# A window attention kernel whose values lie in DRAM with chunks and channels innermost, stored in pieces by two engines

## The chip, the core and the metric

The kernel runs on one core of a Trainium2 chip. The core has five engines that run side by side and are kept in step by semaphores: TensorE (PE) multiplies matrices, VectorE (DVE), ScalarE (ACT) and GpSimd (POOL) work on elements, and SyncE (SP) issues transfers. Transfers between SBUF (on the chip, 128 partitions) and DRAM are carried out by 16 DMA engines. The metric is the device time of one execution, in microseconds (us), where less is better.

## The reference

The input is 16 images of 64 x 64 positions with 256 channels, float32. Two layers run one after the other, each as `x = x + layer(groupnorm(x))`:

```python
# layer 0: linear attention, 8 heads of 32 channels
q, k, v = split(gn(x) @ w_qkv)
q = softmax(q, over a head's channels) * SCALE;  k = softmax(k, over all positions)
x = x + ((k @ v^T) @ q) @ w_out
# layer 1: each position attends to the 7 x 7 positions around it, zero padded
q, k, v = gn(x) @ Wq + bq, gn(x) @ Wk + bk, gn(x) @ Wv + bv
scores = q . (k_window + emb);   x = x + softmax(scores) . v_window
```

The values of layer 1 are what this change is about: `v` is computed for all positions, and every position needs the values of its 49 neighbours, with zeros beyond the image's edge.

## The kernel before, in words

The images are worked through one after the other, in four stages. (1) `layer0` does the linear attention. (2) The group norm of layer 1 is folded into the weights; `positional` computes terms for the position embedding, `store_rings` writes them to DRAM (L658), and `values` computes the values strip by strip and stores them to DRAM (L677, L680, L685, L690). (3) `keys_queries` computes keys and queries for a half of the heads (`hg`), and PSUM is emptied by ACT and DVE into `kaug` and `qq` (L703, L619, L621). (4) `local_attention` computes scores, exponentials and the weighted sums (L760, L768, L791) for that half. Stages 3 and 4 run twice.

The 4096 positions are kept in eight strips of 512. Seven of them are blocks of 8 columns by 64 rows, shifted by 3 so that they match the units of the window scheme. Strip 0 holds the image's two edges, 5 columns on the left and 3 on the right; `block_order` puts these into four groups of 16 rows, within a group the 5 left columns first.

Values go through DRAM because a product with the values needs positions in the partitions in another arrangement than the one in which they are computed. `vpad` is zero padded and has nine units of 8 columns, 72 rows each (nine chunks of 8 rows). Strip `s` is stored as unit `s` by one DMA of 512 KB. Strip 0 belongs to the units 0 and 8 and is stored by eight small DMAs (L690). The zeros around the image are written once, at the start, by 40 small DMAs (L399 to L401). There are two `vpad`, for even and odd images.

`load_window` brings the two units that a step of the attention needs back into SBUF, as `vw`. A DMA moves one unit and one half of the channels: 64 partitions (the 64 positions of a chunk), and for each of them nine chunks with 128 channels (288 KB, in runs of 512 B). Four such DMAs make a window, and two windows are in flight.

The order on PE, ACT, DVE and SP is the order of the program text (`manual_schedule`), so an engine that waits holds up all that follows on it. Around the change it is, for one image: `positional`; the bias of the values; `store_rings` (16 DMAs on SP); `values` for the strips 2, 3, 4, 5, then `load_rings(0)` (8 DMAs on SP, L665 and L666), then `values` for 6, 7, 1, 0; the folding of the key and query biases (L612 on PE, L614 on DVE); two windows loaded; a half of the next image loaded (L463); `keys_queries`; `local_attention`.

Value tiles come from a pool of four buffers that the other stages use too (`work`). A tile that takes a buffer waits until the buffer's last user is done, a store included:

```python
work = ctx.enter_context(tc.tile_pool(name="work", bufs=4))
v4 = work_tile(f"v4_{b}_{s}")
```

The DMAs of the program use eight completion semaphores in turn. A DMA is issued only when the one eight places before it in the program's order has landed.

Of the kernel before, what the change touches and what calls it, by code (L numbers as in the profile page):

```python
# [10 lines left out]
F32 = mybir.dt.float32  # L11
# [8 lines left out]
P = 128  # L20
W = 64
# [19 lines left out]
UNITS = (1, 2, 3, 0)  # L41
KEYED = (2, 3, 4, 5, 6, 7, 1, 0)
ORDER = (3, 4, 5, 6, 7, 1, 2, 0)
EDGE = (5, 3)


def block_order():

    pos = np.arange(NT).reshape(W, W)
    edge = [pos[16 * g : 16 * g + 16, a:e].ravel() for g in range(4) for a, e in ((0, EDGE[0]), (W - EDGE[1], W))]  # L50
    inner = [pos[:, 8 * u - PAD : 8 * u - PAD + 8].ravel() for u in range(1, NB - 1)]
    return np.concatenate(edge + inner)

# [6 lines left out]
def shape_constants():  # L60

    p = np.arange(P)
    c = np.zeros((P, C_COLS), np.float32)
    c[:, C_GRP : C_GRP + P] = (p[:, None] // 8 == p[None, :] // 8) / 8.0
    slot = p % 64
    r = np.arange(RING)
    off = (slot[:, None] - r[None, :]) % RING
    for hg in range(2):
        dyn = (slot >= 32 + 16 * hg) & (slot < 48 + 16 * hg)
        sel = (off[:, :, None] == np.arange(KS)) & dyn[:, None, None]  # L70
        c[:, C_DSEL + 112 * hg : C_DSEL + 112 * (hg + 1)] = sel.reshape(P, -1)
# [10 lines left out]
    blocks = onehot.reshape(2 * RING, WP, NB, 8).transpose(0, 2, 1, 3).reshape(2 * RING, -1)  # L82

    far = np.where((np.arange(RING)[:, None] - np.arange(W)[None]) % RING >= KS, -BIG, 0.0)
    ring = np.broadcast_to(far[:, None, :], (RING, W, W)).reshape(RING, NT)
    return c, onehot, np.ascontiguousarray(blocks), ring.astype(np.float32)


class Net:
# [266 lines left out]
def attention_fast(tc, io, ok):  # L356
# [3 lines left out]
    with ExitStack() as ctx:  # L360
# [28 lines left out]
        xc, xt, out, vpad, pos = io["xc"], io["xt"], io["out"], io["vpad"], io["pos"]  # L389
        B = xc.shape[0]  # L390
        with tc.tile_pool(name="zeros", bufs=1) as zp:
            zero = zp.tile([P, 8 * C], F32, tag="zero", name="zero")
            nc.gpsimd.memset(zero, 0.0)
            last = WP - PAD - W
            for v in vpad:
                rows = v.rearrange("a r w c -> a r (w c)")
                for r0, m in ((0, PAD), (WP - last, last)):
                    for a in range(NB):
                        nc.sync.dma_start(rows[a, r0 : r0 + m], zero[:m])  # L399
                nc.sync.dma_start(v[0, PAD : PAD + W, :PAD].rearrange("r w c -> r (w c)"), zero[:W, : PAD * C])  # L400
                nc.sync.dma_start(v[NB - 1, PAD : PAD + W, PAD:].rearrange("r w c -> r (w c)"), zero[:W, : last * C])  # L401
            far = zp.tile([W, 8 * C], F32, tag="far", name="far")
            nc.gpsimd.memset(far, -BIG)
            for d in pos:
                for i in range(2):
                    part = d[:, RING + 8 * i : RING + 8 * i + 8].rearrange("a s h w -> a (s h w)")
                    nc.sync.dma_start(part, far)
# [8 lines left out]
        for k in kaug:  # L416
            for ab in range(2):
                nc.gpsimd.memset(k[64 * ab : 64 * ab + 32], 0.0)
                nc.sync.dma_start(k[64 * ab + 32 : 64 * ab + 64].rearrange("p a b c -> p (a b c)"), io["blocks"])
        w2 = cp.tile([P, 2, C], F32, tag="w2", name="w2")  # L420


# [59 lines left out]
        def pieces(s):  # L482


            if s:
                yield s, 0, 8, 8 * s - PAD, lambda a: a.rearrange("p (r w) -> p r w", w=8)
                return
            for u, p0, m, n0, w in ((0, PAD, EDGE[0], 0, 0), (NB - 1, 0, EDGE[1], 16 * EDGE[0], W - EDGE[1])):

                def view(a, m=m, n0=n0):  # L490
                    part = a.rearrange("p (g n) -> p g n", g=4)[:, :, n0 : n0 + 16 * m]
                    return part.rearrange("p g (r w) -> p g r w", w=m)

                yield u, p0, m, w, view

        def by_rows(a, like):

            return a.rearrange("p (g r) w -> p g r w", g=4) if len(like.shape) == 4 else a

        def layer0(b, x, xn, mean, rstd, xtok, ready):  # L500

# [136 lines left out]
        def positional(i, pair):  # L638


            for a in range(2):
                for hg in range(2):
                    rows = slice(64 * a + 32 * hg, 64 * a + 32 * hg + 32)
                    image = placed(qq[32 * hg : 32 * hg + 32, 0], hg)
                    for _, _, m, w, view in pieces(pair[a]):
                        src = view(single[i][rows])
                        evacuate(i % 2, by_rows(image[:, :, w : w + m], src), src, bias[rows, 4:5])

        def store_rings():

# [17 lines left out]
        def values(b, s, x):  # L668

            pv, _ = banks()  # L670
            v4 = work_tile(f"v4_{b}_{s}").rearrange("p (t c) -> p t c", c=C)
            for i in range(2):
                pi = pv[i].rearrange("p (t c) -> p t c", c=C)
                for t in range(2):
                    n0 = s * 512 + (2 * i + t) * P
                    for k in range(2):
                        nc.tensor.matmul(pi[:, t], x[k][:, n0 : n0 + P], wv[:, k], start=(k == 0), stop=(k == 1))  # L677
            for i in range(2):
                pi = pv[i].rearrange("p (t c) -> p t c", c=C)
                nc.vector.tensor_tensor(v4[:, 2 * i : 2 * i + 2], pi, bv.unsqueeze(1).to_broadcast([P, 2, C]), ALU.add)  # L680
            v = vpad[b % 2]
            line = 8 * C
            if s:
                row = v[s, PAD, 0]
                nc.sync.dma_start(bass.AP(row.tensor, row.offset, [[C, P], [RING * line, 4], [1, C]]), v4)  # L685
                return
            for u, w, m, p0 in ((0, PAD, EDGE[0], 0), (NB - 1, 0, EDGE[1], 16 * EDGE[0])):
                for t in range(4):
                    row = v[u, PAD + 16 * t, w]
                    nc.sync.dma_start(  # L690
                        bass.AP(row.tensor, row.offset, [[line, 16], [C, m], [1, C]]), v4[p0 : p0 + 16 * m, t]
                    )

        def keys_queries(b, hg, x):

            for what in range(2):
                for i in range(0, NS, 2):
# [12 lines left out]
                    for a in range(2):  # L710
                        for h in range(4):
                            rows = slice(h * HD, (h + 1) * HD)
                            d0 = 64 * (h % 2)
                            for u, p0, m, w, view in pieces(pair[a]):
# [5 lines left out]
                                evacuate(engines[a], by_rows(dst, src), src, bias[rows, 2 * what + hg : 2 * what + hg + 1])  # L720

        def load_window(b, hg, t):

# [2 lines left out]
            v = vpad[b % 2]  # L726
            for j in range(2):
                for e, u in enumerate((2 * t + 2 * j, 2 * t + 1)):
                    row = v[u, 0, 0, hg * P : (hg + 1) * P]
                    src = bass.AP(row.tensor, row.offset, [[C, 64], [64 * C, NB], [1, P]])  # L730
                    nc.sync.dma_start(vw[64 * e : 64 * e + 64, j], src)
            return vw

        def local_attention(b, hg, x, y, vw, after_scores, between):
# [64 lines left out]
            def finish(t):  # L799
# [6 lines left out]
                for j in range(2):  # L806
# [11 lines left out]
                    for s in (2 * t + j, (2 * t + j + 1) % NS):  # L818
                        for _, p0, m, w, view in pieces(s):

                            a, e = max(w, w0), min(w + m, w0 + 8)
                            if a < e:
                                xv, yv = (view(i[hg][:, strip(s)])[..., a - w : e - w] for i in (x, y))
                                nc.gpsimd.tensor_tensor(yv, xv, by_rows(add[:, :, a - w0 : e - w0], xv), ALU.add)  # L824

            groups = [(i, g) for i in range(4) for g in range(5)]
            held = None
# [130 lines left out]
def attention_general(tc, io):  # L958

    nc = tc.nc  # L960
    with ExitStack() as ctx:
# [42 lines left out]
        def strip(s):  # L1004
            return slice(s * 512, (s + 1) * 512)
# [12 lines left out]
        def regroup(back):  # L1018


            for k in range(2):
# [3 lines left out]
                for u in range(NB):  # L1025
# [6 lines left out]
                            c = part[:, :, w - w0 : w - w0 + m]  # L1032
                            nc.vector.tensor_copy(c if back else a, a if back else c)
                    else:
                        m, n0, w = (EDGE[0], 0, 0) if u == 0 else (EDGE[1], 16 * EDGE[0], W - EDGE[1])
                        part = strips[:, strip(0)].rearrange("p (g n) -> p g n", g=4)[:, :, n0 : n0 + 16 * m]
                        c = part.rearrange("p g (r w) -> p g r w", w=m)
                        a = flat.rearrange("p (g r) m d -> p g r m d", g=4)[:, :, :, w % RING : w % RING + m, w // RING]
# [293 lines left out]
```

## Time and profile before

| What | Value |
|---|---|
| Median of 3 runs | 6140.36 us (6137.88 to 6141.98) |
| The profiled execution's own time | 6124.67 us |
| Its span | 6122.9 us |
| PE, DVE, ACT, POOL busy | 89%, 48%, 39%, 17% of the span |
| Granted clock of TensorE, mean | 0.964 of full speed |
| DMA | 536.12 MB, 88 GB/s on the mean |
| Packets under 512 B, under 2 KB, all | 276240, 703504, 772876 |

The span is the time from the first to the last instruction of the program in the profiled execution. An engine is busy when one of its instructions runs; issuing a transfer doesn't count as busy. The profile names an instruction by its line in the kernel (L685), its engine, and the tiles it writes and reads (`vpad<-v`: a store of values into `vpad`). SPq is the queue of SyncE, where the transfers are issued, and "issue" is a wait for nothing that the profile shows. The chain is found backwards from the last instruction, at each step to what released it. The line numbers below are those of the kernel before.

### The profile page before, as it was taken

Reading aid. Unit: us, or ns where it says so; the run is one execution under the profiler, and the core shown is the slowest. Engines: PE = TensorE matmul, PEld = TensorE weight load, DVE = VectorE, ACT = ScalarE, POOL = GpSimd, SP = SyncE. Lnnn points to the kernel's source line nnn. Section 1 sums busy time; section 2 is a strip of 40 time slices with the busy share of each in tenths; the row PEclk is TensorE's granted clock in tenths of the full one; section 3 lists DMA queues with packets and bytes.
Section 4 is the critical chain, followed back from the end, with each engine's and each line's share of the span. In section 5 each row is a group of like instructions: output and inputs, shape, how many; then the busy total and the mean of one; then the engine's idle time right before and its main releaser. Section 6 shows DMA issues by size and latency. Waiting matters only on the chain.

```text
span 6122.9 us, 171756 instructions
## 1 busy us (share of the span) xinstructions
PE 5477.6 (89%) x76913; PEld 3748.6 (61%) x76913; DVE 2963.6 (48%) x5034; ACT 2358.4 (39%) x3233; POOL 1029.9 (17%) x1945
## 2 busy tenths in 40 slices
PE   4989999898998989889898998988989999898997
PEld 2565665655656556665666656566565665656656
DVE  2544545545355454554544554454544545445354
ACT  0251443515335153351623425244252443515335
POOL 2012120211202112021120201212012120211202
PEclk9999999999999999999999999999999999999999
DMA  4341723416244252442515434163341723417234
GB/s 114 83 96 37 138 77 87 104 44 137 59 93 108 50 121 58 104 98 64 115 49 116 92 79 101 43 126 87 84 96 37 136 79 86 103 37 145 59 79 81
DMA packets 772876, 536.12 MB, mean 88 GB/s; under 512 B 276240, under 2 KB 703504, under 8 KB 769552
## 3 DMA queue, kind: packets, MB, share of 16 engines
q1 hardware_dynamic: 772128, 525.04, 38.8%
q8 instruction: 605, 9.91, 0.7%
q14 instruction: 143, 1.17, 0.1%
HBM read 357.02 MB, written 167.90 MB: 86 GB/s over the span
## 4 chain that ended last, share of the span: by engine, by line
PE 79%; ACT 6%; DMA 5%; SPq 4%; issue 4%; DVE 2%; POOL 0%; ACTq 0%; DVEq 0%; POOLq 0%
PE pd L760 15%; PE ps L791 15%; PE pd L514 14%; PE ps L532 7%; ACT qq L619 5%; PE pd L703 4%; PE pd L587 4%; PE ps L587 4%; PE ps L703 3%; PE pd L677 3%; PE ps L677 3%; PE ps L630 2%; DMA vpad<-v 2%; PE ps L546 2%; DMA vw<-vpad 2%
## 5 line engine op out<-in xcount | busy, mean ns | idle before, releaser
L768 ACT ACTIVATE e<-pd 128x896 f32<-128x896 f32 (+2 forms) x1152 | 926.5, 839 | 1078.3 <-PE pd L760 1077.3
L760 PE MATMUL pd<-qq,kaug 64*64 64x224 f32 (+5 forms) x27648 | 1044.8, 293 | 313.0 <-ACT qq L619 152.6
L760 PEld LDWEIGHTS pd<-qq,kaug 64*64 64x64 f32 x27648 | 918.9, 139 | 453.0 <-ACT qq L619 179.1
L514 PE MATMUL pd<-wqkv,img 128*128 128x512 f32 x2048 | 923.0, 595 | 1.6 <-DVE img L283 1.6
L791 PE MATMUL ps<-e,ones 128*32 128x112 f32 (+1 forms) x18432 | 835.6, 253 | 58.5 <-issue 57.9
L791 PE MATMUL ps<-e,vw 128*32 128x112 f32 (+1 forms) x18432 | 838.9, 256 | 54.0 <-issue 53.5
L804 DVE STREAM_TRANSPOSE r<-ps 128x512 f32<-128x512 f32 x256 | 168.7, 696 | 1415.1 <-PE ps L791 1415.1
L619 ACT ACTIVATE qq<-ps,bias 32x512 f32<-32x512 f32 (+2 forms) x544 | 370.1, 725 | 759.2 <-PE ps L630 711.6
L518 ACT ACTIVATE eq<-pd 128x1024 f32<-128x1024 f32 x256 | 261.9, 1023 | 943.5 <-PE pd L514 943.4
L451 POOL TENSOR_TENSOR others<-others,rc 128x16 f32<-128x16 f32 x256 | 113.0, 441 | 3045.1 <-DVE rc L809 3045.1
L514 PEld LDWEIGHTS pd<-wqkv,img 128*128 128x128 f32 x2048 | 372.6, 191 | 380.2 <-issue 352.8
L791 PEld LDWEIGHTS ps<-e,vw 128*32 128x32 f32 x18432 | 494.4, 111 | 139.9 <-issue 101.9
L791 PEld LDWEIGHTS ps<-e,ones 128*32 128x32 f32 x18432 | 536.8, 112 | 68.8 <-issue 67.9
L521 DVE TENSOR_REDUCE qz<-eq 128x16 f32<-128x512 f32 x256 | 175.5, 685 | 830.0 <-ACT eq L518 830.0
L532 PE MATMUL ps<-xtok,eq 128*128 128x257 f32 x2048 | 486.1, 380 | 0.0
L532 PEld LDWEIGHTS ps<-xtok,eq 128*128 128x128 f32 x2048 | 386.1, 190 | 149.0 <-issue 107.2
L824 POOL TENSOR_TENSOR img<-img,r 128x320 f32<-128x320 f32 (+1 forms) x512 | 421.5, 843 | 165.2 <-DVE rc L809 161.4
L619 ACT ACTIVATE kaug<-ps,bias 32x192 f32<-32x192 f32 (+2 forms) x384 | 196.8, 551 | 633.3 <-PE ps L703 630.0
L621 DVE TENSOR_SCALAR qq<-ps,bias 32x512 f32<-32x512 f32 x384 | 351.7, 916 | 8.7
L473 DVE BATCH_NORM_STATS2 st<-img 128x6 f32<-128x512 f32 x512 | 321.2, 677 | 66.4 <-DMA img<-in_xc 66.3
L524 POOL TENSOR_TENSOR eq<-eq,qr 128x512 f32<-128x512 f32 x256 | 274.7, 1073 | 30.7 <-DVE qr L523 1.2
L621 DVE TENSOR_SCALAR qq<-pd,bias 32x512 f32<-32x512 f32 x256 | 236.0, 922 | 29.7 <-PE pd L703 24.8
(126 smaller groups left out, 6269.8 us busy)
## 6 DMA issues: line engine op xcount, KB each, us to landing
vw<-vpad SPq DMA_DIRECT2D x512, 288.0 KB
img<-in_xc SPq DMA_DIRECT2D x256, 256.0 KB
xtok<-in_xt SPq DMA_DIRECT2D x64, 1024.0 KB
out<-img SPq DMA_DIRECT2D x256, 256.0 KB
vpad<-v SPq DMA_DIRECT2D x112, 512.0 KB
qq<-pos SPq DMA_DIRECT2D x128, 256.0 KB
qq<-in_ring SPq DMA_DIRECT2D x128, 256.0 KB
pos<-qq SPq DMA_DIRECT2D x256, 112.0 KB
```

The costliest lines, as they stand in the source:

```text
L473: nc.vector.bn_stats(st[:, k, s], x[k][:, strip(s)])
L514: nc.tensor.matmul(ps[:, t], xn[k][:, n0 : n0 + P], n.wqkv_sb[:, k, : 2 * C], start=(k == 0), stop=(k == 1))
L532: nc.tensor.matmul(pc[hg][:, : C + 1], eq[p][:, t, C + hg * P : C + (hg + 1) * P], xtok[p // 4][:, 2 * (p % 4) + t], start=(p == 0 and t = ...
L587: nc.tensor.matmul(py[co], w2[:, hg, co * P : (co + 1) * P], qq[:, hg, strip(s)], start=(hg == 0), stop=(hg == 1),)
L619: nc.scalar.activation(dst, src, AF.Identity, bias=bias)
L621: nc.vector.tensor_scalar(dst, src, bias, None, ALU.add)
L677: nc.tensor.matmul(pi[:, t], x[k][:, n0 : n0 + P], wv[:, k], start=(k == 0), stop=(k == 1))
L703: nc.tensor.matmul(ps[a], wgt[:, k, hg * P : (hg + 1) * P], x[k][:, strip(pair[a])], start=(k == 0), stop=(k == 1),)
L760: nc.tensor.matmul(to, kaug[pl][rows, u, 8 * c : 8 * c + 8].rearrange("p r w -> p (r w)"), q, start=True, stop=True,)
L768: nc.scalar.activation(e, ps[:, :, : 2 * m], AF.Exp)
L791: nc.tensor.matmul(dst, ones if to is zs[j] else vw[:, j, c, h * HD : (h + 1) * HD], pr, start=False, stop=(c == NB - 1),)
L824: nc.gpsimd.tensor_tensor(yv, xv, by_rows(add[:, :, a - w0 : e - w0], xv), ALU.add)
```

## The change

The diff has four parts.

1. `vpad` is laid out anew: unit, half of the channels, position within a chunk (64), chunk (9), channel (128). The source of a window load is then one run of nine chunks with 128 channels, 4608 B, for each partition.
2. The zeros are written over all of both `vpad`, 9 DMAs for each, 128 partitions and 4608 B a partition.
3. A unit's values are stored by six DMAs: for each half of the channels three pieces of the partitions (40, 64 and 24 of them, for a chunk begins with the padding of 3 rows and so doesn't begin where a tile does). The pieces of the first half are issued by SP, those of the second half by ACT. They have runs of 512 B.
4. The edge strip is ordered by rows, each row with its 3 right columns and then its 5 left ones (`EDGE` is 3), so that it looks like the other strips. It is multiplied by a mask for the left and one for the right edge (`edge`, a new constant) into two tiles of the pool, and both are stored as whole units, with zeros in the other columns. All that reads or writes strip 0 takes its columns by the new order (`pieces`, in the evacuations and in `local_attention`).

```diff
-EDGE = (5, 3)
+EDGE = 3
...
-    edge = [pos[16 * g : 16 * g + 16, a:e].ravel() for g in range(4) for a, e in ((0, EDGE[0]), (W - EDGE[1], W))]
+    edge = [np.concatenate([pos[:, W - EDGE :], pos[:, : 8 - EDGE]], 1).ravel()]
...
             for v in vpad:
-                rows = v.rearrange("a r w c -> a r (w c)")
-                for r0, m in ((0, PAD), (WP - last, last)):
-                    for a in range(NB):
-                        nc.sync.dma_start(rows[a, r0 : r0 + m], zero[:m])
-                nc.sync.dma_start(v[0, PAD : PAD + W, :PAD].rearrange("r w c -> r (w c)"), zero[:W, : PAD * C])
-                nc.sync.dma_start(v[NB - 1, PAD : PAD + W, PAD:].rearrange("r w c -> r (w c)"), zero[:W, : last * C])
+                rows = v.rearrange("u h n c d -> (u h n) (c d)")
+                for a in range(NB):
+                    nc.sync.dma_start(rows[P * a : P * (a + 1)], zero)
...
+        edge = cp.tile([P, 2], F32, tag="edge", name="edge")
+        nc.sync.dma_start(edge, io["edge"])
...
-            for u, p0, m, n0, w in ((0, PAD, EDGE[0], 0, 0), (NB - 1, 0, EDGE[1], 16 * EDGE[0], W - EDGE[1])):
+            cut = [(s, 0, 8, 8 * s - PAD)] if s else [(NB - 1, 0, EDGE, W - EDGE), (0, EDGE, 8 - EDGE, 0)]
+            for u, p0, m, w in cut:
+                yield u, p0, m, w, lambda a, p0=p0, m=m: a.rearrange("p (r w) -> p r w", w=8)[:, :, p0 : p0 + m]
...
             v = vpad[b % 2]
-            line = 8 * C
-            if s:
-                row = v[s, PAD, 0]
-                nc.sync.dma_start(bass.AP(row.tensor, row.offset, [[C, P], [RING * line, 4], [1, C]]), v4)
-                return
-            for u, w, m, p0 in ((0, PAD, EDGE[0], 0), (NB - 1, 0, EDGE[1], 16 * EDGE[0])):
-                for t in range(4):
-                    row = v[u, PAD + 16 * t, w]
-                    nc.sync.dma_start(
-                        bass.AP(row.tensor, row.offset, [[line, 16], [C, m], [1, C]]), v4[p0 : p0 + 16 * m, t]
-                    )
+
+            cuts = ((0, 64 - 8 * PAD, 8 * PAD, 0), (64 - 8 * PAD, P - 8 * PAD, 0, 1), (P - 8 * PAD, P, 0, 2))
+            parts = [(s, v4)]
+            if s == 0:
+                parts = []
+                for i, u in enumerate((0, NB - 1)):
+                    one = work_tile(f"v4_{b}_{s}_{u}").rearrange("p (t c) -> p t c", c=C)
+                    nc.vector.tensor_scalar(one, v4, edge[:, i : i + 1], None, ALU.mult)
+                    parts.append((u, one))
+            for u, vt in parts:
+                for hg, queue in enumerate((nc.sync, nc.scalar)):
+                    for p0, p1, n0, c in cuts:
+                        row = v[u, hg, n0, c]
+                        place = bass.AP(row.tensor, row.offset, [[NB * P, p1 - p0], [2 * P, 4], [1, P]])
+                        queue.dma_start(place, vt[p0:p1, :, hg * P : (hg + 1) * P])
...
-                    row = v[u, 0, 0, hg * P : (hg + 1) * P]
-                    src = bass.AP(row.tensor, row.offset, [[C, 64], [64 * C, NB], [1, P]])
-                    nc.sync.dma_start(vw[64 * e : 64 * e + 64, j], src)
+                    nc.sync.dma_start(vw[64 * e : 64 * e + 64, j], v[u, hg])
...
-    io["vpad"] = [dram.tile([NB, WP, 8, C], F32, tag=f"vpad{i}", name=f"vpad{i}") for i in range(2)]
+
+    io["vpad"] = [dram.tile([NB, 2, 64, NB, P], F32, tag=f"vpad{i}", name=f"vpad{i}") for i in range(2)]
```

More of the change, by code (lines that the diff above doesn't have):

```diff
@@ L82, in shape_constants @@
     blocks = onehot.reshape(2 * RING, WP, NB, 8).transpose(0, 2, 1, 3).reshape(2 * RING, -1)
+    left = p % 8 >= EDGE
+    edge = np.stack([left, ~left], 1).astype(np.float32)
     far = np.where((np.arange(RING)[:, None] - np.arange(W)[None]) % RING >= KS, -BIG, 0.0)
     ring = np.broadcast_to(far[:, None, :], (RING, W, W)).reshape(RING, NT)
-    return c, onehot, np.ascontiguousarray(blocks), ring.astype(np.float32)
+    return c, onehot, np.ascontiguousarray(blocks), ring.astype(np.float32), edge
 class Net:
@@ L391, in attention_fast @@
         with tc.tile_pool(name="zeros", bufs=1) as zp:
-            zero = zp.tile([P, 8 * C], F32, tag="zero", name="zero")
+            zero = zp.tile([P, NB * P], F32, tag="zero", name="zero")
             nc.gpsimd.memset(zero, 0.0)
-            last = WP - PAD - W
             for v in vpad:
-                rows = v.rearrange("a r w c -> a r (w c)")
-                for r0, m in ((0, PAD), (WP - last, last)):
-                    for a in range(NB):
-                        nc.sync.dma_start(rows[a, r0 : r0 + m], zero[:m])
-                nc.sync.dma_start(v[0, PAD : PAD + W, :PAD].rearrange("r w c -> r (w c)"), zero[:W, : PAD * C])
-                nc.sync.dma_start(v[NB - 1, PAD : PAD + W, PAD:].rearrange("r w c -> r (w c)"), zero[:W, : last * C])
+                rows = v.rearrange("u h n c d -> (u h n) (c d)")
+                for a in range(NB):
+                    nc.sync.dma_start(rows[P * a : P * (a + 1)], zero)
             far = zp.tile([W, 8 * C], F32, tag="far", name="far")
@@ L482, in pieces @@
         def pieces(s):
-            if s:
-                yield s, 0, 8, 8 * s - PAD, lambda a: a.rearrange("p (r w) -> p r w", w=8)
-                return
-            for u, p0, m, n0, w in ((0, PAD, EDGE[0], 0, 0), (NB - 1, 0, EDGE[1], 16 * EDGE[0], W - EDGE[1])):
[L490 to L498, printed above, removed]
+            cut = [(s, 0, 8, 8 * s - PAD)] if s else [(NB - 1, 0, EDGE, W - EDGE), (0, EDGE, 8 - EDGE, 0)]
+            for u, p0, m, w in cut:
+                yield u, p0, m, w, lambda a, p0=p0, m=m: a.rearrange("p (r w) -> p r w", w=8)[:, :, p0 : p0 + m]
         def layer0(b, x, xn, mean, rstd, xtok, ready):
@@ L646, in positional @@
                         src = view(single[i][rows])
-                        evacuate(i % 2, by_rows(image[:, :, w : w + m], src), src, bias[rows, 4:5])
+                        evacuate(i % 2, image[:, :, w : w + m], src, bias[rows, 4:5])
         def store_rings():
@@ L681, in values @@
             v = vpad[b % 2]
-            line = 8 * C
-            if s:
-                row = v[s, PAD, 0]
-                nc.sync.dma_start(bass.AP(row.tensor, row.offset, [[C, P], [RING * line, 4], [1, C]]), v4)
-                return
-            for u, w, m, p0 in ((0, PAD, EDGE[0], 0), (NB - 1, 0, EDGE[1], 16 * EDGE[0])):
-                for t in range(4):
-                    row = v[u, PAD + 16 * t, w]
-                    nc.sync.dma_start(
-                        bass.AP(row.tensor, row.offset, [[line, 16], [C, m], [1, C]]), v4[p0 : p0 + 16 * m, t]
-                    )
+            cuts = ((0, 64 - 8 * PAD, 8 * PAD, 0), (64 - 8 * PAD, P - 8 * PAD, 0, 1), (P - 8 * PAD, P, 0, 2))
[12 more added lines that the diff above has]
+                        queue.dma_start(place, vt[p0:p1, :, hg * P : (hg + 1) * P])
         def keys_queries(b, hg, x):
@@ L719, in keys_queries @@
                                     dst = kaug[h // 2][d0 : d0 + HD, u, PAD : PAD + W, p0 : p0 + m]
-                                evacuate(engines[a], by_rows(dst, src), src, bias[rows, 2 * what + hg : 2 * what + hg + 1])
+                                evacuate(engines[a], dst, src, bias[rows, 2 * what + hg : 2 * what + hg + 1])
         def load_window(b, hg, t):
@@ L823, in finish @@
                                 xv, yv = (view(i[hg][:, strip(s)])[..., a - w : e - w] for i in (x, y))
-                                nc.gpsimd.tensor_tensor(yv, xv, by_rows(add[:, :, a - w0 : e - w0], xv), ALU.add)
+                                nc.gpsimd.tensor_tensor(yv, xv, add[:, :, a - w0 : e - w0], ALU.add)
             groups = [(i, g) for i in range(4) for g in range(5)]
@@ L1034, in regroup @@
                     else:
[L1035 to L1038, printed above, removed]
+                        j0, m, w = (EDGE, 8 - EDGE, 0) if u == 0 else (0, EDGE, W - EDGE)
+                        c = strips[:, strip(0)].rearrange("p (r w) -> p r w", w=8)[:, :, j0 : j0 + m]
+                        a = flat[:, :, w % RING : w % RING + m, w // RING]
                         nc.vector.tensor_copy(c if back else a, a if back else c)
@@ L1319 @@
         arrays[name] = np.ascontiguousarray(inputs[given])
-    arrays["cpk"], arrays["onehot"], arrays["blocks"], arrays["ring"] = shape_constants()
+    arrays["cpk"], arrays["onehot"], arrays["blocks"], arrays["ring"], arrays["edge"] = shape_constants()
     io = {
```

## The prediction

> **What bounds the kernel now.** I read the page's busy shares first, then the chain that ended last, its pieces in time for two images, the queue of SyncE (SP) in one image, the list of waits and the start. TensorE (PE) is busy for 89% of the span, so a gain can only come from its idle 645 us, and anything that stops PE is paid in full. Page, parts 1 and 4:
> ```profile
> PE 5477.6 (89%) x76913; PEld 3748.6 (61%) x76913; DVE 2963.6 (48%) x5034; ACT 2358.4 (39%) x3233; POOL 1029.9 (17%) x1945
> PE 79%; ACT 6%; DMA 5%; SPq 4%; issue 4%; DVE 2%; POOL 0%; ACTq 0%; DVEq 0%; POOLq 0%
> ```
> DMA and SP's queue hold 9% of the chain, which looks like what this change is after. The pieces of two images (start, length, what) say otherwise. In the first the chain runs through the value stores and the window loads, in the second through PE and ScalarE (ACT):
> ```profile
> 989.40 3.45 PE pd L677 x16
> 1019.49 11.99 DMA vpad<-v
> 1038.45 8.73 DMA vw<-vpad
> 1053.33 1.79 PE pd L760 x39
> ...
> 2488.42 3.45 PE pd L677 x16
> 2542.21 0.74 ACT qq L619
> 2552.35 2.53 PE pd L760 x39
> ```
> From the first value product (L677) to the full run of scores (L760) both take 63.93 us. The DMA path only ties with the queries' evacuation on ACT; shortening it wins nothing there. SP in the second image (start, length, what):
> ```profile
> 2490.64 9.29 SPq L658 DMA_DIRECT2D pos<-qq  x16
> 2500.03 3.99 SPq L685 DMA_DIRECT2D vpad<-v  x4
> 2514.28 3.30 SPq L666 DMA_DIRECT2D qq<-in_ring  x1
> 2517.68 4.02 SPq L685 DMA_DIRECT2D vpad<-v  x3
> 2521.79 8.28 SPq L690 DMA_DIRECT2D vpad<-v  x8
> 2530.11 7.80 SPq L731 DMA_DIRECT2D vw<-vpad  x8
> ```
> Four value stores go out, then the eight loads of the rings (L665/L666, from 2504.21), then the rest. The rings block the queue until 2517.6. By the trace's semaphore counts they land one per 1.9 us, from 2512.58 to 2525.69; the next three stores land at 2526.8, 2528.2 and 2529.5. Nobody needs these early today. What is due early is this (timeline, last brackets: idle before, and releaser):
> ```profile
> 2516.09 0.69 DVE L680 TENSOR_TENSOR v<-ps,bvn 128x512 f32<-128x512 f32 x1 [1.03 <-PE ps L677]
> 2516.70 0.15 DVE L614 TENSOR_TENSOR bias<-biases,pd 128x2 f32<-128x2 f32 x1
> 2517.81 3.70 PE L703 MATMUL pd<-img,w 128*128 128x512 f32 x8 [0.26 <-DVE bias L614]
> 2524.98 2.75 ACT L619 ACTIVATE kaug<-ps,bias 32x512 f32<-32x512 f32 x4 [33.18 <-PE ps L703]
> ```
> VectorE (DVE) finishes the last values at 2516.78, makes the two biases, and these release the key products. Whatever is put on DVE between L680 and L614 delays PE directly. ACT is idle for 33 us there.
>
> [...] window loads (64 partitions, 288 KB) land one per 1.5 us, 196 GB/s, image loads (128 partitions, 256 KB) one per 0.62 us, 420 GB/s; and the position fill, 64 partitions with 8 KB runs, also gets 512 KB in 2.54 us, 206 GB/s. So long runs should not quicken the window loads. [...] here the last small store, with nothing ahead, took 1.94 us from issue to landing.
>
> **The change part by part**, in the times of the image at 2488.42.
>
> Window loads: the same 512 DMAs and bytes, runs of 512 B become 4608 B. [...] first use is at 2554.8 and eight loads started by 2536 end by 2548. Worth nothing by itself. PE's waits marked "issue" at L791 (111.4 us) and L760 (72.8 us) fall mostly into window loads, together with instruction fetches. Their cost with fewer, longer packets isn't shown: from -184 us (gone) to +184 (doubled); I take 0, since the engines' time hardly changes.
>
> Stores: 15 DMAs an image on SP become 27 on SP and 27 on ACT, in 512 B runs. The zero strip makes two full units, so 2 MB of the second half-stage's stores become 2.5 MB. A store before (512 KB) lands per 1.4 us, small ones per 0.2. A unit's six DMAs: 512 KB at half the run; between 1.6 us and 3 us[...]; I take 2.1. All DMAs of the program take eight completion semaphores in turn, and each waits for the one eight before it; that now ties ACT's stores to SP's.
>
> Zero strip: two DVE multiplications of 128x1024 into new work tiles. L283 takes 0.56 us for 512 elements from SBUF undisturbed, so 1.1 us each. They stand exactly between L680 and L614. Their tiles come from the pool of four that the eight value tiles use: the first takes the buffer of the fifth unit stored (s=6), the second that of the sixth (s=7), and each must wait until all six stores of that unit have landed. Those are issued on SP behind the rings. Step by step:
> - ring stores to 2499.9 as now; the first four units land at 2504.2 + 3 x 2.1 = 2510.5, say 2511.2 (now 2510.4), so value tiles five to eight find their buffers in time;
> - the rings land 0.8 us later than now, plus 0.6 for ACT's three stores that mix in: 2527.1;
> - unit five's SP stores stand behind them in the ring: 2528.6. The first multiplication ends at 2529.7;
> - unit six: its second store waits for the last ring load, and its last three, on ACT, for unit five's stores: issued 2528.3 to 2530, 0.55 each, landed with about 2 us at 2531.4. The second multiplication ends at 2532.5;
> - biases and 16 small products, 1.1 us as now: key products at 2533.7, against 2517.81: **+15.9 us an image**, 16 images 254 us.
>
> PE has nothing to do meanwhile: the key product's bank is the biases' own. Everything later shifts with it. ACT's in-order queue holds all 27 stores ahead of the key evacuation; by the same eight-deep order the last is issued at about 2535, and the evacuation, 7.2 us behind the key products, is due at 2541. That cover of 6 us hides ACT; once gone, each further us costs one. Window loads then start at 2536, against first use at 2570.
>
> Edge strip: evacuations and the POOL additions keep their elements (192 and 320) and count, with another stride: 0 (bounds -1 to +1 us an image; the queries' evacuation on ACT is the one on the path).
>
> Start: 40 small zero stores hold SP from 17.43 to 61.06:
> ```profile
> 17.43 0.30 SPq L399
> ...
> 60.19 0.87 SPq L401
> 61.16 0.85 SPq L407
> 75.59 9.01 DMA img<-in_xc
> ```
> They become 18 stores of 576 KB from 128 partitions. At 512 KB per 1.4 us that is 18 x 1.57 + 2, so landed at 47 where now the last lands at 64.7: -17 us, once. At 206 GB/s it would be +3. One more tiny load: 0.
>
> Sum: 254 - 17 = +237 us on the profiled execution of 6124.67 (span 6122.9). The median of the runs is 6140.36, 0.26% above; I add to that: **6377, given as 6375**.
>
> TensorE's clock: the granted share was 0.93 and 0.90 in two attention stretches of this image and 1.00 in the value stage. A rest of 16 us before them may lift it; from 0 to 4 us of each 65 us stretch, 7%, so 0 to -8 us an image. Nothing in the trace shows that the share follows short rests, and it stays low through waits of this size, so I take 0.
>
> **The rivals.**
> - Faster (3%): the stores land before the multiplications need them, so no stall, and the shorter DMA path pays. For: 9% of the chain, and less work for the DMA engines. Against: the tie at 63.93, and that SP reaches unit five after 2517.6 even now, while DVE wants its buffer at 2516.8. It decides at a landing by 2516.8; then -17 at the start, and up to -184 of the issue waits: 5940 to 6123, most likely near 6100.
> - ACT becomes the bound (10%): if units take 3 us and more, 27 stores end after 2541 and evacuation starts late. 20 to 26 us an image, 6445 to 6540.
> - A short stall (8%): ACT's ring overtakes the loads and the engines share better; the rings are hardly delayed and unit six lands right behind unit five. 8 to 10 us an image, 6250 to 6285.
> - No difference (2%): a short stall paid back by the issue waits, about 6140.
>
> **How the numbers follow.** My case has 77%: 11 to 20 us an image, 176 to 320, less 17, give or take 20 of the issue waits and the clock: 6280 to 6460. Range 6275 to 6465, which leaves the tail of the ACT case and the faster one outside. 0.2% either way is what a measurement can tell from no change. Faster 0.03, same 0.02, slower 0.95.
>
> **What would show it.** DVE idle before the new multiplications, released by a DMA of the value stores, some 12 and 2 us an image; key products waiting on the bias for about 16 us more; ACT with DMA issues until after the rings land; window loads still 1.4 to 1.5 us apart; first image load issued some 17 us sooner. A DVE that waits less than 5 us, or window loads twice as fast with fewer issue waits, would make the forecast wrong.

## The result, and the profile after

The changed kernel takes 6504.55 us (median of 4 runs, 6497.53 to 6513.0), against 6141.17 us before (4 runs): 1.0596 times as long, with a 95% interval of 1.0574 to 1.0617. The prediction was 6375 us with a range up to 6465. The sign and the place were right, and the size was too small by a third: 363 us were lost, not 235.

The page of the kernel after, its span, its busy shares and the two queues of DMAs (q1 is SP's, q10 is ACT's; packets, MB, share of the engines):

```profile
span 6511.2 us, 172551 instructions
PE 5558.4 (85%) x76913; PEld 3802.1 (58%) x76913; DVE 2983.2 (46%) x5066; ACT 2368.3 (36%) x3233; POOL 1034.6 (16%) x1945
q1 hardware_dynamic: 521936, 504.08, 32.4%
q10 hardware_dynamic: 79200, 37.77, 2.3%
```

PE has the same number of matrix products, and its share fell from 89% to 85%: its time outside them grew from 645 to 953 us, and the products themselves last 81 us longer. DVE has 32 instructions more, the two masks of each image. The chain on this page follows only a few per cent of the span, so it can't be compared with the one shown before. The list of waits can (waiting engine, tile and line; releaser; us in total, times, longest):

```profile
PE pd L602 <- DVE bias L604: 365.4, 16, 23.9
DVE v L679 <- DMA vpad<-v: 274.2, 17, 19.2
DVE v L670 <- DMA vpad<-v: 198.4, 44, 10.8
PE ps L783 <- issue: 108.0, 69, 3.6
PE pd L752 <- issue: 51.0, 47, 3.3
```

The lines are those of the new kernel: L602 and L604 are the small products and the biases (before L612, L614), L670 adds the bias to the values (L680), L679 is the new mask, L783 the weighted sum (L791), L752 the scores (L760). Read from the top, they tell the story: once in each image (16 times) PE waits some 23 us for a bias. The bias stands behind the masks on DVE. The masks wait 17 us an image for value stores, and, which the prediction had excluded, the value tiles themselves wait another 12. The last two rows were 111.4 and 72.8 us before: the issue waits of PE fell by 25 us in all, most of it at the scores.

Now one image, the same one as in the prediction. Its first value product starts at 2624.15 (before: 2488.26), so 135.89 us are to be added to the times of the prediction's image. First SP's queue (start, length, what). L648 are the ring stores, L686 the value stores, L655 and L656 the ring loads:

```profile
2626.57 18.80 SPq L648 DMA_DIRECT2D pos<-qq  x16
2645.46 6.60 SPq L686 DMA_DIRECT2D vpad<-v  x12
2652.17 0.33 SPq L655 DMA_DIRECT2D qq<-pos  x1
...
2661.46 2.85 SPq L656 DMA_DIRECT2D qq<-in_ring  x1
2664.40 12.01 SPq L686 DMA_DIRECT2D vpad<-v  x12
```

The sixteen ring stores took 9.29 us before and take 18.80 now. SP's own waits say why:

```profile
SPq L648 <- DMA vpad<-v: 132.9, 77, 5.9
```

Before, no ring store waited for a value store. Now they do so 77 times in all, some five of the sixteen in each image, for 8.3 us an image. Its queue holds no value store at that point: those are ACT's. The eight completion semaphores are given out in the order into which the instructions of all engines were put, and ACT's stores of the first units stand there among SP's ring stores. (Before, where SP issues them all, the numbers 100 to 107 come in turn through all 1900 DMAs of the trace.) In the records of this image a ring store is issued at 2637.85, as a store of ACT lands at 2637.83. That store had itself been issued at 2636.03, for it waited for its value tile.

Then DVE (start, length, line, what; in brackets the idle time before and what ended it):

```profile
2638.23 0.69 DVE L670 TENSOR_TENSOR v<-ps,bvn 128x512 f32<-128x512 f32 x1 [1.10 <-PE ps L667]
2648.93 1.29 DVE L670 TENSOR_TENSOR v<-pd,bvn 128x512 f32<-128x512 f32 x2 [10.00 <-DMA vpad<-v]
...
2673.96 1.47 DVE L679 TENSOR_SCALAR v<-v,edge 128x1024 f32<-128x1024 f32 x2 [16.89 <-DMA vpad<-v]
2675.34 0.15 DVE L604 TENSOR_TENSOR bias<-biases,pd 128x2 f32<-128x2 f32 x1
```

The fifth value tile waits 10 us for the stores of the first unit, which land at 2648.81. That costs nothing more by itself, since the masks wait for a later event: the ring loads land one after the other until 2672.91 (by the trace's semaphore counts), units five and six right behind them from 2673.14 to 2674.55, and the masks start at 2673.96.

Last, what follows on PE and ACT:

```profile
2675.55 1.04 PE L602 MATMUL pd<-gnm,wqn 128*64 128x1 f32 x16 [23.02 <-DVE bias L604]
2676.84 6.43 PE L697 MATMUL pd<-img,w 128*128 128x512 f32 x8 [0.26 <-DVE bias L604]
...
2686.75 2.75 ACT L609 ACTIVATE kaug<-ps,bias 32x512 f32<-32x512 f32 x4 [59.02 <-DMA vw<-vpad]
```

The key products start 52.69 us after the first value product; before it was 29.55, and the prediction said 45.4 (2533.7 less 2488.26). And the first eight of them take 6.43 us, where before they took 3.70. The windows of the trace show TensorE's granted clock (the third number from the end, ahead of the DMA share) while PE idles and while these products run, first after, then before:

```profile
2640.00:2676.00 36.00, 12.98 (x81) 11.19 (x79) 6.69 (x11) 0.00 (x0) 0.00 (x0) 0.71 0.90 168
2676.80:2684.00 7.20, 7.16 (x11) 3.10 (x12) 0.68 (x1) 0.00 (x0) 0.00 (x0) 0.61 0.69 188
2684.00:2709.00 25.00, 23.31 (x55) 10.04 (x53) 22.85 (x32) 19.66 (x31) 0.00 (x0) 1.00 0.56 157
```

```profile
2517.80:2525.00 7.20, 7.19 (x17) 3.34 (x18) 3.40 (x5) 0.02 (x1) 0.00 (x0) 1.00 1.05 148
```

In 7.2 us eleven products were started in place of seventeen, at a clock of 0.61 in place of 1.00; soon after, it is 1.00 again.

The stages of all 16 images (means in us, worked out from the starts of the first products of each stage in the trace) give the sum. "Start" is the first query product of image 0; "values" runs from the first value product to the first key product, "keys, first half" from there to the first score, and "attention, half" from the first score of a half to PE's next work.

| kernel | span | start | values | keys, first half | attention, half |
|---|---|---|---|---|---|
| before | 6122.9 | 96.8 | 29.5 | 30.5 | 70.9 |
| after | 6511.2 | 76.4 | 52.5 | 32.8 | 71.1 |

Of 388.3 us, 16 x 23.0 = 368 are the values and 16 x 2.3 = 37 the keys; 20 are won at the start, and 4 are left for all the rest.

### The profile page after: what moved, and what is told of

Its sections match the earlier page's. It is cut to its first block, busy times and chain, and to the rows that moved or that the text cites. A ratio compares the mean times of both kernels' runs of the same rounds, so it can differ in the third digit from the quotient of the medians.

```text
span 6511.2 us, 172551 instructions
## 1 busy us (share of the span) xinstructions
PE 5558.4 (85%) x76913; PEld 3802.1 (58%) x76913; DVE 2983.2 (46%) x5066; ACT 2368.3 (36%) x3233; POOL 1034.6 (16%) x1945
## 5 line engine op out<-in xcount | busy, mean ns | idle before, releaser
L760 ACT ACTIVATE e<-pd 128x896 f32<-128x896 f32 (+2 forms) x1152 | 927.3, 839 | 1082.7 <-PE pd L752 1067.4
L752 PE MATMUL pd<-qq,kaug 64*64 64x140 f32 (+5 forms) x27648 | 1071.5, 298 | 283.4 <-ACT qq L609 152.9
L752 PEld LDWEIGHTS pd<-qq,kaug 64*64 64x64 f32 x27648 | 943.4, 142 | 423.1 <-ACT qq L609 179.4
L783 PE MATMUL ps<-e,vw 128*32 128x112 f32 (+1 forms) x18432 | 848.2, 259 | 54.8 <-issue 54.2
L783 PE MATMUL ps<-e,ones 128*32 128x112 f32 (+1 forms) x18432 | 841.7, 255 | 54.4 <-issue 53.8
L783 PEld LDWEIGHTS ps<-e,vw 128*32 128x32 f32 x18432 | 499.7, 113 | 143.1 <-issue 105.7
L783 PEld LDWEIGHTS ps<-e,ones 128*32 128x32 f32 x18432 | 542.5, 114 | 66.9 <-issue 66.4
L609 ACT ACTIVATE kaug<-ps,bias 32x320 f32<-32x320 f32 (+2 forms) x384 | 201.6, 556 | 1036.9 <-PE ps L697 743.3
L602 PE MATMUL pd<-gnm,wqn 128*64 128x1 f32 x256 | 16.6, 248 | 365.4 <-DVE bias L604 365.4
```

Source lines behind the costliest of these rows:

```text
L609: nc.scalar.activation(dst, src, AF.Identity, bias=bias)
L752: nc.tensor.matmul(to, kaug[pl][rows, u, 8 * c : 8 * c + 8].rearrange("p r w -> p (r w)"), q, start=True, stop=True,)
L760: nc.scalar.activation(e, ps[:, :, : 2 * m], AF.Exp)
L783: nc.tensor.matmul(dst, ones if to is zs[j] else vw[:, j, c, h * HD : (h + 1) * HD], pr, start=False, stop=(c == NB - 1),)
```

## The experiments

Three theories were held against each other. A: the masks take buffers of the common pool, and so wait for stores that stand behind the ring loads. B: the DMA engines are too slow for the many short pieces, whoever waits. C: the second issuer alone does it, by the semaphores that it shares with SP. Two edits and their combinations tell them apart, and then single parts were put into the kernel before. "After" and "before" name the base of each diff. The ratios are to runs of the kernel before that were made together with each experiment (medians 6136.45 us for the first four, 6139.12 us for the last three).

### The masks get buffers of their own (from after)

```diff
-                    one = work_tile(f"v4_{b}_{s}_{u}").rearrange("p (t c) -> p t c", c=C)
+                    one = tail.tile([P, 2, 512], F32, tag="tail", name=f"v4_{b}_{s}_{u}")
+                    one = one.rearrange("p a n -> p (a n)").rearrange("p (t c) -> p t c", c=C)
```

The tiles come from the pool of the attention's last step, which is not in use at that time.

> The changed kernel, with the two masked edge tiles in buffers of the attention's tail pool, which nothing uses in this stage, in place of the four work buffers. Theory A (two waits on buffers and one shared order of semaphores): the masks follow the last value addition at once, so key products start some 36 us after the first value product in place of 52.7. ScalarE's in-order queue is late next: its last stores still wait for the ring loads, so its key evacuation starts at about 53 us in place of 62.6. About 10 us an image less than the changed kernel: 6350 us (6300 to 6400). Theory B (the DMA engines are simply too slow for 54 short-run stores an image): the stores are as late, and the time stays near 6505. Theory C (only that ScalarE issues stores hurts): also near 6505.

Measured: 6221.58 us (2 runs), 1.0142 of before (1.0113 to 1.0171), below even the range that was expected. The values fell from 52.5 to 35.1 us an image, so three quarters of the 23 us hang on this one choice of pool. What was expected to take over did not: in this kernel no store of ACT waited for a ring load (some five ring loads an image waited for value stores instead), and ACT's key evacuation followed the products without delay. DVE, with the masks now directly behind the values:

```profile
2539.13 1.29 DVE L670 TENSOR_TENSOR v<-pd,bvn 128x512 f32<-128x512 f32 x2 [9.70 <-DMA vpad<-v]
...
2547.10 1.42 DVE L680 TENSOR_SCALAR v<-v,edge 128x1024 f32<-128x1024 f32 x2
```

ACT in the same image:

```profile
2519.62 31.72 ACTq L687 DMA_DIRECT2D vpad<-v  x27
2558.60 2.75 ACT L609 ACTIVATE kaug<-ps,bias 32x512 f32<-32x512 f32 x4 [40.35 <-PE ps L698]
```

The masks no longer wait (no bracket), ACT waits for PE and not the other way round. The fifth value tile still waits 9.70 us for the first unit's stores, and the ring stores still take 18.5 us. That is now on the path: it is most of the 5.6 us that are left, as the kernel with both edits, below, shows.

### All stores issued by SP (from after)

```diff
-                for hg, queue in enumerate((nc.sync, nc.scalar)):
+                for hg, queue in enumerate((nc.sync, nc.sync)):
```

> The changed kernel, with all 54 stores of an image issued by SyncE. Theory A: the ring stores take their 9.3 us again, in place of 18.8, but SyncE then issues 24 value stores of 0.55 us ahead of the ring loads, which land by 44 to 46 us after the first value product; units five and six land behind them, and the masked tiles still wait for their buffers: key products at 49 to 51 us in place of 52.7, 6450 to 6490 us. Theory C (only that ScalarE issues stores hurts): back to 6130 to 6180. Theory B (engines too slow): near 6505.

Measured: 6439.85 us (2 runs), 1.0498 (1.0467 to 1.0529), 10 us below the range of A; values 51.0. So C falls as the whole cause: without the second issuer all but 1.5 us of the loss in the values is still there in each image. SP's queue and, below it, DVE in one image whose first value product is at 2582.65:

```profile
2585.06 9.27 SPq L648 DMA_DIRECT2D pos<-qq  x16
2594.42 13.40 SPq L686 DMA_DIRECT2D vpad<-v  x24
2607.93 0.32 SPq L655 DMA_DIRECT2D qq<-pos  x1
...
2618.06 21.53 SPq L686 DMA_DIRECT2D vpad<-v  x30
```

```profile
2628.47 0.75 DVE L679 TENSOR_SCALAR v<-v,edge 128x1024 f32<-128x1024 f32 x1 [17.31 <-DMA vpad<-v]
2631.04 0.75 DVE L679 TENSOR_SCALAR v<-v,edge 128x1024 f32<-128x1024 f32 x1 [1.82 <-DMA vpad<-v]
```

The ring stores are back at 9.27 us, which shows that it was ACT's stores that stretched them. But the 24 stores ahead of the ring loads now take SP 13.40 us, 0.56 each, where the four large ones took 3.99, a wait for a value tile included. The ring loads begin 25.3 us after the first value product (before 16.0, after 28.0) and land until 44.1 (before 37.4, after 48.8). Either way they are late, by the rings waiting on another engine's stores or by the number of issues; and here the second mask waits for unit six by itself, as the prediction had put it.

The values are not the whole difference from the changed kernel. The profiled spans differ by 77 us, of which 24 are the values; most of the rest lies in the attention, 69.4 us a half in place of 71.1. No run shows why.

### Only the first four units by SP (from after)

```diff
-                for hg, queue in enumerate((nc.sync, nc.scalar)):
+                for hg, queue in enumerate((nc.sync, nc.sync if s in KEYED[:4] else nc.scalar)):
```

> The changed kernel, with the stores of the first four units issued by SyncE alone and those of the others by SyncE and ScalarE as changed. Theory A: ring stores are in one piece again (9.3 us), ring loads land by 44 us and not 48.8, key products start at about 48.5 us in place of 52.7: 6440 us (6400 to 6470). Theory B: near 6505. Theory C: ScalarE still issues for the last units, so near 6505 as well.

Measured: 6460.95 us (2 runs), 1.0532 (1.0491 to 1.0573), within what was expected; values 49.5. The ring stores take 9.29 us here too. But in the image looked at the ring loads land until 47.2 us after the first value product and not by 44 as expected, later than with SP alone: its 24 stores ahead of them took 15.97 us in place of 13.40. ACT's stores of the next units, which follow in the order of the semaphores, may be why; that was not shown. The values are nonetheless 1.5 us shorter than with SP alone, since the stores of units five and six, shared by two issuers, follow the last ring load sooner: from its landing to the key products it is 3.8 us on the mean, against 6.5. The time as a whole does not follow the values here, and its interval overlaps that of the kernel with SP alone, so the order of the two kernels is not settled.

### Both edits (from after)

The masks' own buffers and all stores on SP, as in the two diffs above.

> The changed kernel, with both edits: all stores issued by SyncE, masked tiles in buffers of the tail pool. Theory A: no engine but SyncE waits for a store in this stage, so what is left of the change is the masks on VectorE (1.5 us an image), the colder start of TensorE if any, and the shorter fill at the start (-20 us once): 6155 us (6130 to 6200). Window loads start at about 55 us and land by 68, when they are due. Theory B: at least 6400. Theory C: as sp_only.

Measured: 6166.98 us (5 runs), 1.0054 (1.0038 to 1.0071); values 31.1, keys 32.1. B falls: the same bytes in the same pieces, to the same places, and the values are 1.5 us an image from those before. DVE shows what these are, and that the masks wait for nothing:

```profile
2514.66 0.69 DVE L670 TENSOR_TENSOR v<-ps,bvn 128x512 f32<-128x512 f32 x1 [0.49 <-PE ps L667]
2515.39 1.42 DVE L680 TENSOR_SCALAR v<-v,edge 128x1024 f32<-128x1024 f32 x2
```

The two masks take 1.42 us on the path to the biases. The key products that follow start slowly here too, 1.7 us an image, though PE waits for the bias only this long:

```profile
2516.93 0.65 PE L602 MATMUL pd<-gnm,wqn 128*64 128x1 f32 x16 [1.72 <-DVE bias L604]
2517.83 5.40 PE L698 MATMUL pd<-img,w 128*128 128x512 f32 x8 [0.26 <-DVE bias L604]
```

That accounts for the 31 us that this kernel still loses: 24 for the masks and 27 for the slow start, less 20 at the start. The window loads land 60 to 69 us after the first value product, as in the changed kernel, and nobody is late for that.

So the 23.0 us of the values divide like this. With two issuers, the masks' pool is worth 52.5 - 35.1 = 17.4; the second issuer is then worth another 4.1, and the masks' own work 1.5. In the other order the second issuer is worth 1.5 and the pool 19.9. They are not independent: both delay the same ring loads.

### The zeros written whole (from before)

```diff
-            zero = zp.tile([P, 8 * C], F32, tag="zero", name="zero")
+            zero = zp.tile([P, NB * P], F32, tag="zero", name="zero")
...
-                rows = v.rearrange("a r w c -> a r (w c)")
-                for r0, m in ((0, PAD), (WP - last, last)):
...
+                rows = v.rearrange("a r w c -> (a r w c)").rearrange("(n f) -> n f", f=NB * P)
+                for a in range(NB):
+                    nc.sync.dma_start(rows[P * a : P * (a + 1)], zero)
```

> The kernel before, with one part of the change alone: the zeros are written over all of both value tensors by 18 stores from 128 partitions (4608 B a partition), not around the image by 40 small ones. If the 20 us that the changed kernel gains at its start come from this part, the first queries start at about 76 us in place of 96.8 and all else stays: 6116 us (6108 to 6124), ratio about 0.9967. If they come from something else in the change, no difference.

Measured: 6118.74 us (9 runs), 0.9961 (0.9947 to 0.9975). This part of the change by itself wins 20 us: the first query product comes at 76.1 us in place of 96.8. The start is the only stage of the table that is shorter in the changed kernel.

### Window loads in long runs (from before)

```diff
-                    row = v[u, 0, 0, hg * P : (hg + 1) * P]
-                    src = bass.AP(row.tensor, row.offset, [[C, 64], [64 * C, NB], [1, P]])
+                    row = xt[b].rearrange("q p t c -> (q p t c)")
+                    n0 = (2 * u + hg) % 14 * 64 * NB * P
+                    src = row[n0 : n0 + 64 * NB * P].rearrange("(n c d) -> n c d", c=NB, d=P)
```

The windows come from the tokens of the input, in runs of 4608 B, and not from the stored values, so the attention weights other numbers than the values. Stores, counts and bytes are those of before.

> The kernel before, with window loads alone in runs of 4608 B: they read the same number of bytes from the input tensor of tokens, one run for each partition (so the values that are weighted aren't the computed ones, and the loads don't depend on the stores). [...] TensorE's waits in the attention stay, and the time is that of before within 0.3%. Rival (long runs free the engines): TensorE's issue waits, 184 us in all, go for a good part: 5960 to 6090.

Measured: 6099.14 us (5 runs, 6094.6 to 6126.2), 0.9929 (0.9909 to 0.9949). This lies between the two expectations. The profiled execution was the slowest of the five (span 6124.4) and shows no gain in any stage: values 29.5, keys 30.5, attention 71.0. Of PE's issue waits, 111.4 and 72.8 us before, the second is 17 us shorter:

```profile
PE ps L792 <- issue: 114.2, 72, 3.3
PE pd L761 <- issue: 55.9, 47, 2.9
```

The loads land 1.3 us apart, where it was 1.5: as little as in the changed kernel. The shorter wait at the scores goes with the long runs: it is 44 to 60 us in the five kernels with the new layout and 67 to 80 in the three that load runs of 512 B. Where the other four runs won 0.4 to 0.7% stays open. That the loads wait for no store here may have a part in it; it was not tried apart.

### The zeros written later (from before)

Both fills, the zeros and the far entries of the position terms, go out behind the first image's loads, as whole stores from two tiles of the attention's last pool.

```diff
-        with tc.tile_pool(name="zeros", bufs=1) as zp:
-            zero = zp.tile([P, 8 * C], F32, tag="zero", name="zero")
...
+        def fill():
+            zero, far = (tail.tile([P, 2, 512], F32, tag="tail", name=i) for i in ("zero", "far"))
...
+            for v in vpad:
+                rows = v.rearrange("a r w c -> (a r w c)").rearrange("(n f) -> n f", f=864)
+                for a in range(12):
+                    nc.sync.dma_start(rows[P * a : P * (a + 1)], zero[:, :864])
...
             xtok = {q: load_tokens(0, q) for q in range(2)}
+            fill()
```

> The kernel before, with both constant fills (zeros of the value tensors, -1e30 of the positions) moved behind the loads of the first image, from tiles of the tail pool, by 24 and 8 stores of 128 and 64 partitions. If the start is bound by SyncE's queue of fills, the first queries start at about 46 to 50 us in place of 96.8, and the fills hide behind the first linear attention: 6090 us (6082 to 6100). If the fills then hold up the later token loads, 5 to 20 us of it come back.

Measured: 6085.45 us (6 runs, 6072.15 to 6091.74), 0.9909 (0.9892 to 0.9926): faster than both kernels, as expected. SP's queue at the start:

```profile
10.06 18.22 SPq L445 DMA_DIRECT2D img<-in_xc  x16
28.69 1.39 SPq L451 DMA_DIRECT2D xtok<-in_xt  x2
30.17 27.06 SPq L640 DMA_DIRECT2D vpad<-zero  x24
58.09 12.20 SPq L644 DMA_DIRECT2D pos<-far  x8
```

The image goes first, and the fills run while PE already works: the first query product comes at 39.8 us, 57 sooner than before and sooner than the 46 to 50 expected.

## Why the prediction was wrong

**Right: the mechanism.** The masks take the buffers of units five and six, whose stores stand behind the ring loads; they hold up the biases, and these the key products. The expected marks are all there: DVE idle ahead of the masks, released by value stores (16.89 us, told some 12 and 2), PE waiting for the bias, PE without other work. Giving the masks other buffers took 17.4 of 23.0 us away.

**Wrong: "ring stores to 2499.9 as now".** This is the step that failed. In the prediction's times they end at 2509.5 (21.2 us after the first value product, not 11.6). The prediction knew that all DMAs take eight semaphores in turn and that this "ties ACT's stores to SP's", but applied it only to the second half of the units. The order in which all engines' DMAs take the semaphores puts ACT's stores of units one to four among the ring stores, so some five of these waited for stores that wait for value tiles. With it falls "value tiles five to eight find their buffers in time" (10.00 us waited), and the last ring load lands at 2537.0 and not at 2527.1 (48.8 us after the first value product, not 38.8): +9.9 us.

**Wrong, the other way: from the rings to the key products.** 6.6 us were told (unit five 1.5 later, unit six after it, two multiplications of 1.1, biases 1.1), and 3.9 were needed. The stores of both units landed together, so the two masks ran back to back at 0.73 us each. +9.9 - 2.7 = +7.2 is the whole miss of this image, 52.69 against 45.4; over 16 images the mean is 23.0 - 15.9 = 7.1, or 114 us.

**Wrong: the clock of TensorE at 0.** The prediction asked whether a rest lifts the clock later, gave "0 to -8 us" and took 0. No lift shows: the attention takes 70.9 and 71.1 us a half, and in its first half the granted clock is 0.97 on the mean before and 0.93 after, in its second 0.92 and 0.91. What a rest costs came at once: in the image above the first key products start 1012, 854, 853, 853, 854, 853, 563 and then 430 ns apart, where before it was 534 and then 429. That is 2.3 us an image on the mean, 37 in all. From the first key product to full pace it took 3.3 to 6.6 us, 4.9 on the mean over the 16 images; before, it took 0.53 us in each. The trace of before shows such a slow start too, at its beginning: the first query products, after PE's wait of 77.66 us for the first image, start 1015, 853, 854, 853, 853, 854, 633 and then 430 ns apart. The prediction had waits of 16 us in its sum and should have charged each with this.

**The sum.** 114 + 37 for these, -3 for the start (told -17, it was -20) and 4 for the rest make, but for rounding, the 151 us between the predicted 237 and the 388 of the spans. The median adds less than was taken: the runs after lie below the profiled one, not 0.26% above, which brings the miss down to some 128 us in the medians.

**Right, or nearly.** Window loads: from 1.5 us apart to 1.3, told 1.4 to 1.5. 288 KB in 1.31 us are 225 GB/s, against 196 before. The issue waits of PE, taken at no change with a bound of 184 us either way, fell by 25 us. Before, 146 of the 184 lay beside packets of 512 B, the size of the window loads', and 149 beside packets of the queues that the page calls "instruction". ACT: its last store was issued at 2678.9, its key evacuation was due at 2686.75, so the second rival (ACT becomes the bound) did not come about, and it did not in the kernel with the masks' own buffers either. The edge strip, told 0: the first half's keys grew by no more than the slow start explains.

**A second issuer.** It saves time of the issues here, 12 stores in 6.60 us on SP where one issuer needs 13.40 for 24. But with the masks' own buffers the kernel with two issuers took 6222 us against 6167 with one, and the 4.1 us an image of the values (65 us) account for it: two in-order queues that take turns at the same eight semaphores wait for each other (SP's ring stores and ring loads 319 us for value stores, and none with one issuer), and that was more than the saving. With the masks in the common pool it was 6505 against 6440, but there the values account for only 24 us.

## What to carry to other kernels

Before a tile is taken from a shared pool, ask which DMA frees its buffer and what stands ahead of that DMA in its queue: a mask of 0.73 us cost 17 us because its buffer was that of a store behind eight loads. When stores go to a second queue, follow the completion semaphores through the order of all engines, not through the text of one, and count the issues as well as the bytes. Price a new idle stretch of TensorE with a slow start of its products on top; here waits of 2 to 23 us cost 1.7 to 2.3 us each.

## What the runs showed of the hardware

- The first products after 23 us of rest take twice as long (854 ns for 429, the very first 1012). In the kernel with both edits, where PE waits for the bias only 1.7 us, they are slow too, 5.40 us for the first eight in place of 3.70: 3.2 us lie there between the last value product and the first key product, with only 32 products of one column in them, and this cost 1.7 us an image. Before, these were 1.8 us, and the products started at full pace.
- SP issues a store of a sixth of a unit in 0.56 us on the mean (24 in 13.40 us). The four whole units before took 3.99 us, a wait for a value tile included: cutting each store into six made this stretch of the queue 3.4 times as long.
- Window loads, 288 KB to 64 partitions, landed 1.3 us apart in runs of 4608 B and 1.5 us apart in runs of 512 B.
